# Three first-layer products split once more, Wq and Wk loaded by quarters, and a rebuilt adapter end in a one-core attention and MLP kernel

## The chip, the core and the metric

The kernel runs on one core of one Trainium2 chip. The metric is the device time of one execution in microseconds (us); a time below is in us unless it says otherwise. Engines are named as in the profile: PE is TensorE's matmul, PEld its weight load, DVE is VectorE, ACT is ScalarE, POOL is GpSimd, SP is SyncE (here it only issues DMAs). L1065 is line 1065 of the kernel before.

## What is computed

There are four sequences of 512 tokens with 512 features, all in float32. Cut to what matters, with `H = 2048`, `BN = 256` and one of three adapters chosen per sequence:

```python
q, k, v = x @ Wq, x @ Wk, x @ Wv
attn = softmax(q @ k.T * 512 ** -0.5)
attn_out = (attn @ v) @ Wp + bp
cms = gelu(attn_out @ cW1 + cb1) @ cW2 + cb2 + one_hot(code)      # 512 -> 2048 -> 512
mod = gelu(concat(attn_out, cms) @ mW1 + mb1) @ mW2 + mb2         # 1024 -> 2048 -> 512
y = clip(x + cms + mod, 0, 1)
h = y + gelu(y @ W_down[e] + b_down[e]) @ W_up[e] + b_up[e]       # adapter e of the sequence
out = (h - mean(h)) / sqrt(var(h) + 1e-5) * ln_w[e] + ln_b[e]
```

## The kernel before, in words

**Pairs and seven products.** The work goes by two pairs of sequences. Most products are done by a seven-product scheme (Strassen's in Winograd's form): the left operand is cut into four blocks, the right operand into four, seven products of sums of blocks take the place of eight, and the results are recombined by additions. In the MLP layers this is done at two levels: each of the seven outer products is itself done as seven. `FIRST_C`, `FIRST` and `SECOND` give the order of the outer products.

**The layer cW1** (`c1_layer`, L1035) has 512 features in and is only partly at two levels. Its outer products run in the order 2, 1, 5, 6, 7, 3, 4. Products 1 and 5 are done by `c1_two_level` (L990), which needs sums of weight blocks (the DRAM tensors `c1_inner`, made once by POOL in `expand_c1`, L217) and sums of token blocks (made on DVE in `c1_operands`, L960). Products 2, 6, 7, 3 and 4 are one-level: two groups of weights `g`, four tiles each, two matmuls of 128x128 by 512 columns per tile (L1065). The results of products 6 and 7 are put together per tile by `combine_first_tile` (L1078): two additions on DVE and a copy on ACT.

**The recombination inside a two-level product** is `seven` (L549). For each of two rows it holds sums in PSUM banks; there are eight banks in all, given out in turn. ACT copies the first product, DVE adds, and `keep` stores each of the four result blocks.

**Where the sums of weights come from.** POOL makes them while the first pair runs: `expansion` for cW1, cW2 and mW1 during attention, `late_expansion` for mW2 during pair 0's mW1 layer (L1131). They go to DRAM and come back through four weight slots `wslot`, which SP fills in the order of use (`fetch` L986, `inner_weights` L374).

**The second layers** (`second_layer`, L1189; matmuls L1215) need differences of blocks of the hidden values; `second_operands` (L1156) has DVE make them, half by half (`LOW`, `HIGH`), some of them beside the last products of the layer before (`after`).

**The start.** Wq and Wk come in by four row blocks each, on SP's and ACT's queues in turn (L120). PE turns all of Wq, then all of Wk (`transposed`, L411); ACT copies them out (L681, L641), DVE makes the eight block sums, and `folded` (L692) multiplies them by seven products (`small_product`, L652; matmuls L659). The first sequence's x is turned after that, and the first product with x is `pair_product` (L590; matmuls L595).

**The adapter** (`adapter`, L1307) is a generator, one step at a time between other work. PE turns the sequence back to rows (L1314), ACT copies it, POOL adds b_up; two down products with gelu follow (L1323, L1330), and then for each of four token tiles an up product (L1335), DVE's addition of the residual (L1343), statistics (L1345, L1347), the root on ACT (L1350), and the normalisation over ACT, DVE and POOL (L1352 to L1368). Pair 0's two adapters run between the products of pair 1's cW1 layer. Pair 1's second sequence runs around the last product of the last layer, its first sequence at the very end, so that nothing covers it.

**What sets the order.** Each engine works through its own list in order, and so do the DMA queues of SP, ACT and POOL. A scheduler places the instructions from the order of the code; `keep_in_program_order` pins some.

Of the kernel before, what the change touches and what calls it, by code (L numbers as in the profile page):

```python
# [18 lines left out]
def kernel(  # L19
# [38 lines left out]
    nc = tc.nc  # L58
# [64 lines left out]
    wq = weight((nc.sync, nc.scalar, nc.sync, nc.scalar), Wq, slot[0])  # L123
    wk = weight((nc.sync, nc.scalar, nc.sync, nc.scalar), Wk, slot[1])
# [12 lines left out]
    x_rows = [load_x(0, nc.scalar, x_places[0])]  # L137
    wv = weight((nc.scalar, nc.scalar), Wv, slot[2])
    x_rows.append(load_x(1, nc.sync, x_places[1]))
# [34 lines left out]


# [19 lines left out]
    def flat(t):  # L195
# [3 lines left out]

    c1_outer = [spill.tile([P, 3, 2, 2, 256], F32, name=f"c1_outer{u}") for u in range(2)]  # L200
    c1_inner = {
        (p, u): spill.tile([P, n], F32, name=f"c1_inner_{p}_{u}")
        for p, n in ((1, 1024), (5, 2048))
# [13 lines left out]
    def expand_c1(u, then):  # L217
# [23 lines left out]
        yield  # L241

# [43 lines left out]
    def expand(unit, raw, pairs, last, then):  # L286
# [40 lines left out]
        if last is not None:  # L327
            yield from plain((2, a12, one), (1, a11, three), (4, a22, two))
            tt(block(last), a12, s2, ALU.subtract)
            then()  # L330
            yield from full((5, one), (7, three), (6, two))
            yield from fourth(block(last), one)
        else:
            yield from plain((2, a12, one))
            tt(a12, a12, s2, ALU.subtract)
            yield from fourth(a12, three)
            yield from plain((1, a11, two), (4, a22, one))
            yield from full((5, one), (7, three), (6, two))
            then()

    def expand_all(units, raw, pairs, last):
        if last is None:
            load_raw(*units[0][:2], units[0][3], raw)
        for n, unit in enumerate(units):

            def then():
                if n + 1 < len(units):
                    load_raw(*units[n + 1][:2], units[n + 1][3], raw)

            yield from expand(unit, raw, pairs, last, then)  # L350
# [19 lines left out]
    def late_expansion():  # L370

        yield from expand_all(m2_units, slot[6:8], (flat(mod[0]), flat(mod[1]), slot[0]), None)
# [38 lines left out]
    def transposed(get, dst, finish=None):  # L411

        ps = [bank("tr_ps") for d in range(4)]
# [5 lines left out]
        for d in range(4):  # L419
            if finish is None:  # L420
                evacuate(dst[:, d, :], ps[d])
            else:
                finish(d, ps[d])
# [228 lines left out]
    def small_product(lhs, rhs, keep, then=None, copy=nc.scalar.copy):  # L652


        def matmuls(p, _, ps, first_):
# [14 lines left out]
            (1, 5, 6, 2, 7, 3, 4), then, copy,  # L670
# [5 lines left out]
    def left_from_psum(t, s):  # L676

        s1, s2, s3, s4 = (s[:, k] for k in range(4))

        def finish(d, ps):  # L680
            nc.scalar.copy(t[:, d, :], ps)  # L681
            c = d % 2
            if d < 2:
                minus(s3[:, c], ps[:, :256], t[:, c, 256:])
            else:
                minus(s2[:, c], ps[:, 256:], s3[:, c])
                add(s1[:, c], ps[:, 256:], t[:, c, 256:])
                minus(s4[:, c], ps[:, :256], s2[:, c])

        return finish  # L690

    def folded(lhs, rhs, w, s):  # L692
# [17 lines left out]
        small_product(lhs, rhs, keep)  # L710
# [71 lines left out]
    def first_operand(pair):  # L782
        xT, t_x = places(pair)
        transposed(chunks(x_rows[2 * pair]), xT[0], right_from_psum(xT[0], sums_in(flat(t_x[0]))))
# [17 lines left out]
    transposed(chunks(wq), wq_t, left_from_psum(wq_t, s_q))  # L802
    transposed(chunks(wk), wk_t, right_from_psum(wk_t, t_k))
    lhs_qk = folded(left_operand(wq_t, s_q), right_operand(wk_t, t_k), w_qk, sums_in(slot[0]))
    first_operand(0)
    load_bias()
    begun = both_operands(0)
    for pair in range(B // 2):
# [59 lines left out]
        if pair == 0:  # L868
            begun = {}
            then = {6: [lambda: first_operand(1)], 4: [lambda: begun.update(both_operands(1))]}  # L870
# [89 lines left out]
    def c1_operands(slots=(0, 1, 2, 3)):  # L960

        at0, at1, t12, t34 = (in_rows[i] for i in slots)
        b11, b12, b21, b22 = at0[:, 0:2, :], at1[:, 0:2, :], at0[:, 2:4, :], at1[:, 2:4, :]
        t1, t2, t3, t4 = t12[:, 0:2, :], t12[:, 2:4, :], t34[:, 0:2, :], t34[:, 2:4, :]

        def inner_sums(k, t):
            s = mod[1][:, 2 * k : 2 * k + 2, :].rearrange("p a (b n) -> p (a b) n", b=2)
            return inner_operands(t, 1, [s[:, i : i + 1, :] for i in range(4)], pinned=True)
# [4 lines left out]
        one = {1: inner_sums(0, b11)}  # L973
        minus(t1, b12, b11)

        def rest():
            one[5] = inner_sums(1, t1)
# [6 lines left out]
        return one, {2: b21, 3: b22, 4: t4, 6: t2, 7: t3}, rest()  # L984
# [5 lines left out]
    def c1_two_level(p, h, rhs):  # L990
# [3 lines left out]
        for g in range(2):  # L994
            w = next_weights()
            if p == 1:
                for m in range(2):
                    at = m * 512 + g * 256
                    fetch(
                        out=w[:, 512 * m : 512 * m + 512].rearrange("p (c n) -> p c n", c=2),  # L1000
                        in_=cW1[0:256, at : at + 256].rearrange("(c p) n -> p c n", p=P),
                    )
                fetch(out=w[:, 1024:], in_=c1_inner[1, g])
            else:
                fetch(out=w, in_=c1_inner[5, g])
# [17 lines left out]
        def keep(g, place, ps):  # L1023
            o, t = place
            tiles, tokens = slice(4 * o + 2 * g, 4 * o + 2 * g + 2), slice(256 * t, 256 * t + 256)
            nc.scalar.copy(h[2 if p == 1 else 3][:, tiles, tokens], halves_of(ps))
            if p == 1:
                done = h[0][:, tiles, tokens]
                add(done, halves_of(ps), done)

        seven(2, matmuls, keep, (1, 5, 6, 2, 7, 3, 4), at=mod[0])
# [3 lines left out]
    def c1_layer(h, rhs, after):  # L1035

        two_level, one_level, rest = rhs
        for p in FIRST_C:
            if p in (1, 5):
                c1_two_level(p, h, two_level[p])  # L1040
                yield
                continue
            for g in range(2):
                w = next_weights()
                if p in (2, 4):
                    k, o = {2: (1, 0), 4: (1, 1)}[p]
# [9 lines left out]
                else:  # L1056
                    s = {3: 2, 6: 0, 7: 1}[p]
                    a = w[:, :1024].rearrange("p (j c n) -> p j c n", j=2, c=2)
                    for j in range(2):
                        fetch(out=a[:, j], in_=c1_outer[j][:, s, g])  # L1060
                    lhs = lambda c, t, a=a: a[:, t // 2, c, (t % 2) * P : (t % 2 + 1) * P]
                for t in range(4):
                    ps = bank(f"c1_{p}")
                    for c in range(2):
                        nc.tensor.matmul(  # L1065
                            ps, lhsT=lhs(c, t), rhs=one_level[p][:, c, :],
# [8 lines left out]
                after(p, g)  # L1075
                yield
# [79 lines left out]
    def second_operands(h):  # L1156
# [19 lines left out]
        def after(p, g):  # L1176

            if (p, g) == (3, 1):
                differences(1, LOW)
                differences(3, LOW)  # L1180
# [4 lines left out]

        ready = []
        return operands, differences, after, ready

    def second_layer(made, src, kept_w, c, last, bias_c, beside):  # L1189

        operands, differences, _, ready = made
        c11, c12, c21, c22 = c
        rhs = ready[0]
        for i, p in enumerate(SECOND):
# [3 lines left out]
            if i == 0:  # L1198
                differences(3, HIGH)
# [92 lines left out]

    def load_adapter(b, w, aff):
        wd = w[:, : NV * BN].rearrange("p (c n) -> p c n", c=NV)
        wu = w[:, NV * BN : NV * BN + NB * V].rearrange("p (c n) -> p c n", c=NB)
        aff = aff[:, : 3 * V].rearrange("p (k n) -> p k n", k=3)
        bd = small.tile([P, NB], F32, name="bd")
        for c in range(NV):
            gathered(wd[:, c, :], wd_rows, idx_d[:, b, c : c + 1])
        for c in range(NB):  # L1300
            gathered(wu[:, c, :], wu_rows, idx_u[:, b, c : c + 1])
            gathered(bd[:, c : c + 1], bd_rows, idx_u[:, b, c : c + 1])
        for i, rows in enumerate((b_up, ln_w, ln_b)):
            gathered(aff[:, i, :], rows, idx_e[:, b : b + 1])
        return wd, wu, bd, aff

    def adapter(b, y, loaded, g, rows, eng, final=False):  # L1307

        wd, wu, bd, aff = loaded

        for t in range(NT):
            ps = bank("res_ps")
            for c in range(NV):
                nc.tensor.transpose(  # L1314
                    ps[:, c * P : (c + 1) * P], y[:, c, t * P : (t + 1) * P], ident
                )
            nc.scalar.copy(rows[:, t, :], ps)
# [198 lines left out]
```

## Time and profile before

| | us |
|---|---|
| median of 3 runs (1192.6 to 1193.76) | 1193.23 |
| the profiled execution, its own time | 1194.26 |
| its span, first to last instruction | 1192.5 |
| PE busy | 1168.9 |
| DVE busy | 883.5 |
| POOL busy | 482.7 |
| ACT busy | 294.9 |

The stages of the profiled execution, from its chain of waits: the start and the attention to about 248, the first cW1 layer from there to 346, cW2 to 431, mW1 to 602, mW2 to 686; then pair 1's cW1 layer with pair 0's adapters to 812, cW2 to 896, mW1 to 1065, mW2 with the second sequence's adapter to 1165, and the last adapter to the end. A row of the chain or of the order of time begins with its start and its length; a row of the waits has the total, the number of times and the longest; a row of groups has the count, the busy total and the mean of one in ns. An f32 matmul appears as two records. A granted clock of 1.00 is full speed.

### The profile page before, as it was taken

The numbers are of one execution on the slowest core, as the hardware profiler recorded it, in microseconds if no ns is written. First come the engines' busy times: TensorE is split into PE (matmuls) and PEld (weight loads), VectorE is DVE, ScalarE is ACT, GpSimd is POOL, SyncE is SP. The second block draws the span as 40 slices with busy tenths as digits, with TensorE's granted clock in tenths as the row PEclk, the third lists the DMA queues.
The fourth block names the chain that finished last, engine by engine and source line by source line (L and its number), as shares of the span: only waits on it lengthen the run. The fifth ranks groups of instructions, "written<-read, shape, count | busy, mean of one in ns | idle before, by whom it ended". The sixth has DMA issues, their size and how long they took to land.

```text
span 1192.5 us, 13167 instructions
## 1 busy us (share of the span) xinstructions
PE 1168.9 (98%) x4809; PEld 894.8 (75%) x4809; DVE 883.5 (74%) x1221; ACT 294.9 (25%) x540; POOL 482.7 (40%) x542
## 2 busy tenths in 40 slices
PE   7999999999999999999999999999999999999996
PEld 6478558747468888888888857447888888888872
DVE  4735565476789867897899837779894588699947
ACT  3234325335520000012310037551000002220014
POOL 4788999988940048870000522110000010124015
PEclk9999999999999999999999999999999999999998
DMA  8743695698756478787737553132735454775601
GB/s 289 277 149 135 245 351 196 218 389 331 262 194 249 176 279 319 283 293 251 241 134 297 177 177 133 54 132 106 293 131 187 166 211 168 219 240 187 228 1 71
DMA packets 78368, 251.50 MB, mean 211 GB/s; under 512 B 7348, under 2 KB 34016, under 8 KB 63456
## 3 DMA queue, kind: packets, MB, share of 16 engines
q1 hardware_dynamic: 54768, 149.96, 35.0%
q0 software_dynamic: 20736, 89.17, 21.2%
q10 hardware_dynamic: 2800, 11.54, 2.5%
q8 instruction: 38, 0.62, 0.2%
q14 instruction: 26, 0.21, 0.1%
HBM read 185.63 MB, written 65.01 MB: 210 GB/s over the span
## 4 chain that ended last, share of the span: by engine, by line
PE 92%; DMA 3%; DVE 2%; POOL 2%; ACT 1%; SPq 1%; issue 0%; ACTq 0%; DVEq 0%; POOLq 0%
PE i L1215 28%; PE i L1131 27%; PE c L1065 10%; PE sum L595 8%; PE sum L659 7%; PE sum L1014 4%; PE down_ps L1323 2%; PE up_ps L1335 2%; DMA wslot<-c_inner 1%; DMA wslot<-in_L_cond_mW 1%; PE tr_ps L416 1%; PE prod_ps L430 1%; PE res_ps L1314 1%; DMA wide<-in_L_cond_Wk 1%; SPq L988 1%
## 5 line engine op out<-in xcount | busy, mean ns | idle before, releaser
L1131 PE MATMUL i<-slot,wslot 128*128 128x256 f32 x1184 | 260.8, 379 | 0.0
L1131 PEld LDWEIGHTS i<-slot,wslot 128*128 128x128 f32 x1184 | 225.0, 190 | 30.6
L1215 PE MATMUL i<-slot,wslot 128*128 128x256 f32 x896 | 202.5, 379 | 0.0
L1215 PEld LDWEIGHTS i<-slot,wslot 128*128 128x128 f32 x896 | 170.2, 190 | 23.1
L906 ACT COPY first<-i 128x256 f32<-128x256 f32 (+1 forms) x56 | 26.8, 479 | 544.9 <-PE i L1215 280.6
L1215 PE MATMUL i<-hidden,wslot 128*128 128x256 f32 x576 | 132.2, 379 | 0.0
L899 DVE TENSOR_TENSOR part<-i,part 128x512 f32<-128x512 f32 (+1 forms) x156 | 90.9, 591 | 43.1 <-PE i L1131 26.6
L1215 PEld LDWEIGHTS i<-hidden,wslot 128*128 128x128 f32 x576 | 109.4, 190 | 16.2 <-issue 1.4
L928 ACT ACTIVATE hidden<-hidden,bias 128x512 f32<-128x512 f32 x128 | 85.2, 716 | 61.8 <-DVE hidden L505 60.7
L1065 PE MATMUL c<-slot,wslot 128*128 128x512 f32 x224 | 97.3, 592 | 0.0
L1065 PEld LDWEIGHTS c<-slot,wslot 128*128 128x128 f32 x224 | 42.5, 190 | 53.1 <-issue 50.5
L1286 POOL DMA_INDIRECT slot<-in_L_cond_W_down,idx_d x12 | 15.5, 1288 | 149.8 <-PE i L1215 88.2
L1286 POOL DMA_INDIRECT slot<-in_L_cond_b_up,idx_e x3 | 4.3, 1420 | 174.1 <-PE i L1131 173.5
L505 DVE TENSOR_TENSOR sum<-sum,wslot 128x512 f32<-128x512 f32 x51 | 35.4, 697 | 36.8 <-PE sum L659 18.7
L190 DVE TENSOR_TENSOR slot<-hidden,slot 128x1024 f32<-128x1024 f32 x48 | 58.4, 1217 | 0.3
L190 DVE TENSOR_TENSOR slot<-hidden 128x1024 f32<-128x1024 f32 x48 | 58.4, 1216 | 0.0
L899 DVE TENSOR_TENSOR part<-i,first 128x512 f32<-128x512 f32 (+1 forms) x62 | 36.3, 589 | 28.6 <-PE i L1131 16.2
L505 DVE TENSOR_TENSOR hidden<-c,hidden 128x512 f32<-128x512 f32 x64 | 43.3, 688 | 15.5 <-PE c L1065 14.3
L659 PE MATMUL sum<-hidden,wslot 128*128 128x256 f32 x232 | 53.5, 380 | 0.4 <-POOL wslot L180 0.4
L284 POOL DMA_DIRECT2D slot<-in_L_cond_mW x24 | 17.9, 753 | 81.4 <-DVE slot L190 80.5
L659 PEld LDWEIGHTS sum<-hidden,wslot 128*128 128x128 f32 x232 | 43.6, 190 | 6.8 <-POOL wslot L180 0.8
L505 DVE TENSOR_TENSOR hidden<-part,hidden 128x2048 f32<-128x2048 f32 x20 | 48.1, 2405 | 0.5
(307 smaller groups left out, 1988.6 us busy)
## 6 DMA issues: line engine op xcount, KB each, us to landing
wslot<-m_kept SPq DMA_DIRECT2D x48, 1024.0 KB
wslot<-m_kept SPq DMA_DIRECT2D x36, 512.0 KB
wslot<-c_kept SPq DMA_DIRECT2D x16, 1024.0 KB
slot<-in_L_cond_mW POOLq DMA_DIRECT2D x24, 512.0 KB
wslot<-in_L_cond_mW SPq DMA_DIRECT2D x24, 512.0 KB
slot<-in_L_cond_cW POOLq DMA_DIRECT2D x16, 512.0 KB
wslot<-in_L_cond_cW SPq DMA_DIRECT2D x32, 256.0 KB
m_kept<-wide POOLq DMA_DIRECT2D x6, 1024.0 KB
```

What stands on the lines that cost most here:

```text
L190: i = eng.tensor_tensor(out_, one, two, ALU.subtract)
L505: nc.vector.tensor_tensor(dst, a, b, ALU.add)
L595: nc.tensor.matmul(ps, lhsT=lhs[p][:, c, r * P : (r + 1) * P], rhs=rhs[p][:, c, :], start=(first_ and c == 0), stop=(c == 1), skip_group_c ...
L659: nc.tensor.matmul(v[:, j, :], lhsT=lhs[p][:, c, j * P : (j + 1) * P], rhs=rhs[p][:, c, :], start=(first_ and j == 0 and c == 0), stop=(c ...
L899: nc.vector.tensor_tensor(dst, ps, other, ALU.add)
L906: nc.scalar.copy(c1, p1)
L928: nc.scalar.activation(block[:, t, :], block[:, t, :], AF.Gelu, bias=bias_c[:, 8 * half + t : 8 * half + t + 1],)
L1014: nc.tensor.matmul(halves_of(ps)[:, j, :], lhsT=a[g][:, at_[q], j * P : (j + 1) * P], rhs=rhs[q][:, 0, :], start=(first_ and j == 0), stop ...
L1065: nc.tensor.matmul(ps, lhsT=lhs(c, t), rhs=one_level[p][:, c, :], start=(c == 0), stop=(c == 1),)
L1131: nc.tensor.matmul(out_ps[:, j, :], lhsT=a[j][q][:, c, :], rhs=now[q][:, c, :], start=(c == 0), stop=(c == 1),)
L1215: nc.tensor.matmul(ps[:, :256], lhsT=a[k // 2][q][:, k % 2, :], rhs=now[q][:, k, :], start=(k == 0), stop=(k == 3),)
L1323: nc.tensor.matmul(ps, lhsT=wd[:, c, n * P : (n + 1) * P], rhs=y[:, c, :], start=(c == 0), stop=(c == NV - 1),)
```

## The change

What it does, by parts:

- **Three more products at two levels**, in pair 1's cW1 layer only (`more`): 2, 6 and 7 beside 1 and 5. Sums of their weights are made in a second part of the late expansion, `expand_c1_late`. In pair 1 the token sums of all five are made on POOL instead of DVE, each ahead of its product (`prepare`). After product 6 or 7, DVE adds a block to h21 and POOL makes h12 or h22 from it. The adapters' steps are put inside the two-level products (`beside`).
- **The start**: Wq on SP's queue and Wk on ACT's, each by quarters of 256 rows and 256 columns. Each quarter of both is turned when it is there, and the products of the fold stand between the quarters, in the order 1, 2, 5, 6, 7, 3, 4; the first x is turned inside the fold. x, Wv and Wp follow on SP's queue. A tiny copy on ACT at the beginning (`touched`) calls for the activation table.
- **The adapters**: b_up is loaded as columns and added to y by ACT (`with_bias`). PE turns y in the up product's own bank, and the two up matmuls add to it, so that statistics and normalisation read PSUM. DVE subtracts the mean and multiplies by ln_w in one operation; ACT multiplies by the reciprocal root and POOL adds ln_b, or, for the last tiles, DVE does both in one.
- **The last adapter** goes by token halves: three of four half-width down products, the up products of tiles 0 and 1, the fourth down product, and tiles 2 and 3. The roots are pinned behind.
- **Half of one difference** of the second layers (`t1`, `LOW`) is made by ACT (a negated copy) and a DMA that adds, on POOL's queue, except in pair 0's cW1 layer; another (`t3`, `LOW`) moves to the second layer's beginning.
- In `expand` the next raw weights are loaded ahead of the last three blocks, and pair 0's mW1 layer takes three steps of the late expansion at a time instead of two.

The core of the diff:

```diff
-    wq = weight((nc.sync, nc.scalar, nc.sync, nc.scalar), Wq, slot[0])
-    wk = weight((nc.sync, nc.scalar, nc.sync, nc.scalar), Wk, slot[1])
+    QUARTERS = ((0, 0), (0, 1), (1, 0), (1, 1))
+    wq = quarters(Wq, slot[0], nc.sync)
+    wk = quarters(Wk, slot[1], nc.scalar)
...
+    def expand_c1_late(raws, sums):
+        units = [(p, u) for p in (2, 6, 7) for u in range(2)]
...
+        def rest():
+            for i, (p, u) in enumerate(units):
+                raw = block_of(i)
+                to = sums[i % 4].rearrange("p (k n) -> p k n", k=4)
+                weight_sums(
+                    raw[:, 0, 0], raw[:, 0, 1], raw[:, 1, 0], raw[:, 1, 1],
+                    *(to[:, k] for k in range(4)),
+                )
+                if i + 4 < len(units):
+                    load(i + 4)
+                nc.gpsimd.dma_start(out=c1_inner[p, u], in_=sums[i % 4])
+                yield
...
     def late_expansion():
-        yield from expand_all(m2_units, slot[6:8], (flat(mod[0]), flat(mod[1]), slot[0]), None)
+        spaces = (flat(mod[0]), flat(mod[1]), slot[0])
+        quarters = lambda tiles: [t[:, at : at + 1024] for t in tiles for at in (0, 1024)]
+        begin, rest = expand_c1_late(quarters(slot[6:8]), quarters(spaces[:2]))
+        yield from expand_all(m2_units, slot[6:8], spaces, None, begin)
+        yield from rest
...
-    transposed(chunks(wq), wq_t, left_from_psum(wq_t, s_q))
-    transposed(chunks(wk), wk_t, right_from_psum(wk_t, t_k))
-    lhs_qk = folded(left_operand(wq_t, s_q), right_operand(wk_t, t_k), w_qk, sums_in(slot[0]))
-    first_operand(0)
+    both_quarters(0, 0)
+    lhs_qk = folded(
+        lhs_q, rhs_k, w_qk, sums_in(slot[0]),
+        {
+            1: [lambda: both_quarters(0, 1), lambda: both_quarters(1, 0)],
+            2: [lambda: both_quarters(1, 1)],
+            6: [lambda: ends.append(first_operand(0))],
+            7: [lambda: ends[0]()],
+        },
+    )
...
         def keep(g, place, ps):
...
+            if p == 2:
+                nc.scalar.copy(h11, z)
+            elif p == 1:
+                nc.scalar.copy(h21, z)
+                add(h11, z, h11)
+            elif p == 5:
+                nc.scalar.copy(h22, z)
+            else:
+                add(h21, z, h21)
+                nc.gpsimd.tensor_tensor({6: h12, 7: h22}[p], h22, h21, ALU.add)
+            if p == 7 and place in ((0, 1), (1, 0)):
+                gelu(h[3], 1, cb1_c, (first_tile, first_tile + 1))
...
+        two = [p for p in FIRST_C if p in ((2, 1, 5, 6, 7) if more else (1, 5))]
...
+                ready[two[i]] = inner_sums(two[i], i % 2, nc.gpsimd if more else None)
...
+            if (p, g) == (3, 0) and not busy:
+                for two in (slice(0, 2), slice(2, 4)):
+                    tc.keep_in_program_order(
+                        nc.scalar.activation(t1[:, two, :], h11[:, two, :], AF.Copy, scale=-1.0)
+                    )
+            elif (p, g) == (3, 1):
...
+                    nc.gpsimd.dma_start(out=t1[:, LOW, :], in_=h12[:, LOW, :], accum_op=ALU.add)
...
+    def up(g, wu, y1, aff, h, t):
+        ps = bank("up_ps")
+        for c in range(NV):
+            nc.tensor.matmul(
+                ps[:, c * P : (c + 1) * P], lhsT=y1[:, c, t * P : (t + 1) * P], rhs=ident,
+                is_transpose=True, start=(c == 0), stop=True, skip_group_check=True,
+            )
+        for n in range(NB):
+            nc.tensor.matmul(
+                ps,
+                lhsT=g[:, n, t * P : (t + 1) * P],
+                rhs=wu[:, n, :],
+                start=False,
+                stop=(n == NB - 1),
+                skip_group_check=True,
+            )
...
+        nc.vector.scalar_tensor_tensor(h, ps, mv[:, 0:1], aff[:, 0, :], ALU.subtract, ALU.mult)
...
+    def normalised(b, h, mv, aff, t, eng, last=False):
+        rstd = small.tile([P, 1], F32, name="rstd")
+        root = nc.scalar.activation(rstd, mv[:, 1:2], AF.Sqrt, bias=eps)
+        if last:
+            tc.keep_in_program_order(root)
+        nc.vector.reciprocal(rstd, rstd)
+        if t == NT - 1 or last and t == NT - 2:
+            nc.vector.scalar_tensor_tensor(h, h, rstd, aff[:, 1, :], ALU.mult, ALU.add)
+        else:
+            nc.scalar.activation(h, h, AF.Copy, scale=rstd)
+            nc.gpsimd.tensor_tensor(h, h, aff[:, 1, :], ALU.add)
+        eng.dma_start(out=out[b, t * P : (t + 1) * P, :], in_=h)
...
+    def last_adapter(b, y, loaded, g, rows, y1, eng):
+        wd, wu, bd, bu, aff = loaded
+        with_bias(y, bu, y1)
+        first_half, second_half = slice(0, 256), slice(256, 512)
+        for n, tokens in ((0, first_half), (1, first_half), (0, second_half)):
+            down(y, wd, bd, g, n, tokens)
+        mvs = [up(g, wu, y1, aff, rows[:, t, :], t) for t in range(2)]
+        down(y, wd, bd, g, 1, second_half)
+        for t in range(NT):
+            if t > 1:
+                mvs.append(up(g, wu, y1, aff, rows[:, t, :], t))
+            normalised(b, rows[:, t, :], mvs[t], aff, t, eng, last=True)
```

## The prediction

> **What bounds the kernel now.** I read the page's busy times first, then what TensorE (PE) waits for, then the chain of waits, and last the order of time at both ends and around the first layer of pair 1.
>
> ```profile
> PE 1168.9 (98%) x4809; PEld 894.8 (75%) x4809; DVE 883.5 (74%) x1221; ACT 294.9 (25%) x540; POOL 482.7 (40%) x542
> ...
> PE tr_ps L416 <- DMA wide<-in_L_cond_Wq: 4.4, 1, 4.4
> PE sum L659 <- ACT hidden L641: 1.6, 1, 1.6
> PE i L1131 <- DMA wslot<-in_L_cond_mW: 1.3, 1, 1.3
> ...
> PE sum L1014 <- DVE sum L505: 0.9, 1, 0.9
> ```
>
> The columns of the waits are total, times and longest, in us. PE is busy for 1168.9 of 1192.5 us. Of the other 23.6, 4.4 is the wait for Wq, 1.6 the wait for its copies, some 11.4 comes after PE's last product (1181.1 to 1192.5), and about 6 is scattered. So only three things shorten this kernel: fewer PE passes, an earlier start, a shorter end. Work taken off VectorE (DVE) elsewhere is worth almost nothing, because DVE hardly ever holds PE up.
>
> **Three products at two levels.** The chain of waits prices both forms of a first-layer product.
>
> ```profile
> 686.29 6.87 PE c L1065 x16
> ...
> 698.34 6.87 PE c L1065 x16
> ...
> 710.61 12.09 PE sum L1014 x56
> ```
>
> The columns are start, length, what. Each f32 product is two records. A one-level product is two such groups of 16 records of 512 columns, 2 x 6.87 = 13.74 us; a two-level one is 56 records of 256 columns, 12.09 us. Products 2, 6 and 7 of pair 1 change over: 3 x 1.65 = 4.9 us of PE removed, on the path. The transposes of the adapters stay as many (16 each), the downs and ups too.
>
> What the new form asks of the others, by its rows: product 6 or 7 needs 8 DVE adds inside the recombination and 8 into h21, 16 x 0.69 = 11.0 us, as much as the 16 adds of its one-level form did, in 1.65 us less. With its share of the adapter (bn_stats 0.69, aggregate 0.18, subtract-and-scale 0.99, reciprocal 0.15 = 2.0 per token tile, against 2.7 before) product 7 loads DVE with 11.0 + 2 x 2.0 = 15.0 us beside 12.09 + 2 x 2.15 = 16.4 us of PE. DVE is covered, by little. POOL gets 8 adds of 1.27 us for each of products 6 and 7 (L1368's row, 128x512) and 4 sums of 0.72 us ahead of each two-level product: 13 of 16 us. By the order of the built kernel the sums for products 2 and 1 stand ahead of the 16 large adapter gathers on POOL's queue, so product 2 does not wait behind some 26 us of gathers (664.6 to 690.4 before). Behind POOL's adds wait DVE's next adds into h21, and ScalarE's (ACT's) gelu of h22; that is due only two products (27 us) later. With 8 banks, the next product's second bank is that of this product's last sum but one; between them lie two to four us of adapter products, except after products 2 and 1. I charge 0.9 us, the size of the one such wait in the rows above. Net **-4.0**; bounds -6.4 (the 1.45 us that PE loses today in 686 to 811 goes too) and 0.
>
> **The start.** Now all of Wq and Wk land before PE can multiply.
>
> ```profile
> 4.39 3.64 PE L416 MATMUL tr_ps<-ident,wide 128*128 128x128 f32 x16 [4.39 <-DMA wide<-in_L_cond_Wq]
> ...
> 8.20 2.92 PE L416 MATMUL tr_ps<-ident,wide 128*128 128x128 f32 x16 [0.16 <-DMA wide<-in_L_cond_Wk]
> ...
> 8.82 1.28 ACT L681 ACT_TABLE_LOAD   x1 [8.82 <-DMA wide<-in_L_cond_Wk]
> ...
> 12.71 2.05 PE L659 MATMUL sum<-hidden 128*128 128x256 f32 x8 [1.59 <-ACT hidden L641]
> ...
> 28.79 3.60 PE L595 MATMUL sum<-hidden,cms 128*128 128x512 f32 x8
> ```
>
> The quarters are the same 2 MB at the same 385 GB/s or so (1 KB rows instead of 2 KB; the cW1 loads with 1 KB rows ran in the stretch at 388). The first pair should land at 4.4, the last near 8.1. The table load (1.28) moves into the wait. Then, in PE's order: 8 transposes at the early 0.23 us, to 6.2; the copies, 0.7, to 6.9; product 1, 8 records at 0.2 to 0.4, to about 9.7; 16 transposes at 0.11 to 0.15, to 11.6; a copy; product 2, 1.73, to 13.7; the last 8 transposes, 0.9, to 14.6; product 5 behind one add of 0.7, and then 5 products (8.6) with x's transposes (1.75 and 1.75) and the bias, to 27.3. The sums (512 wide, 0.69 each, 8 of them) stay ahead from product 6 on. So the pair product starts at 27.3 instead of 28.8: **-1.5**. Bounds: 0, and -5.1 if PE ran from 4.39 with no wait at its later rate (64 x 0.109 + 12.1 + 0.3 = 19.4). x now follows Wq on SP's queue, Wv and Wp behind it; Wv is needed at 46 and Wp at 56 us, 4 MB at 385 GB/s are in by 19. The savings carry through the attention: POOL's chain there (0.4 us of PE waits) starts earlier too, since x lands sooner than today's 16.5 us.
>
> **The end.** PE's work after the last product is unchanged in sum, so its end stays where it is on before's scale, 1181.1.
>
> ```profile
> 1179.09 0.73 ACT L1350 ACTIVATE rstd<-mv,eps 128x1 f32<-128x1 f32 x2
> ...
> 1182.94 0.98 DVE L1352 SCALAR_TENSOR_TENSOR hidden<-hidden,mv,wide 128x512 f32<-128x512 f32 x1
> ...
> 1184.03 1.56 DVE L1356 SCALAR_TENSOR_TENSOR hidden<-hidden,rstd,wide 128x512 f32<-128x512 f32 x1
> ...
> 1185.51 1.74 DVE L1367 TENSOR_TENSOR hidden<-hidden,wide 128x512 f32<-128x512 f32 x1
> ...
> 1188.01 0.33 SPq L1369 DMA_DIRECT2D out<-hidden  x1
> ```
>
> Today the last output is issued 6.9 us after PE's end, and lands 4.5 us later. In the new order the last gelu ends two ups (4.3 us) before PE's end, less 0.7, at 1177.5; the root's table load 1.28, to 1178.8; the roots and scales of tiles 0 and 1 (2 x 1.1), to 1181.0; DVE then does tile 2 (0.69 + 0.18 + 0.99 + 0.15, and about 1.0 for the last), largely behind PE's end, to 1183.2, and tile 3, 2.8, to 1186.0. The residual's add, the shift and one of two affine passes are gone. SP issues at 1186.1: **-2.0**. Bounds -4.0 (tile 2 fully hidden) and 0 (ACT's order makes DVE wait: the roots now stand behind all four gelus).
>
> **The rest.** Pair 0's m1 layer (431 to 602 us) gets POOL's late sums for cW1: 24 x 0.72 = 17 us, 18 DMA issues of 0.6 and some landings, so POOL ends near 565 instead of 533; the next use of its buffers, the sums at 589, has 24 us left. Some 16 more small gathers (columns of b_up), 1.3 us each, fall into POOL's idle 342 to 422. Half of t1 done by ACT and an adding DMA: no cost; it can start near 580, after product 3's gelus, and the sums that read it come after 605. But POOL and DVE disturb each other. The first row is a DVE group beside POOL in 440 to 460 (mean 3,378 ns, where two more of the same shape took 722), the second a POOL addition beside DVE at 524, and the third gives the busy time of PE, PEld, DVE, ACT and POOL in 20 us:
>
> ```profile
> L190 DVE TENSOR_TENSOR slot<-slot,slot 128x512 f32<-128x512 f32 x2 | 6.8, 3378 | 0.0
> ...
> 523.77 2.77 POOL L180 TENSOR_TENSOR wide<-wide 128x256 f32<-128x256 f32 x1
> ...
> 500.00:520.00 20.00, 20.00 (x94) 17.62 (x93) 19.79 (x20) 1.17 (x2) 17.28 (x19) 1.00 0.68 241
> ```
>
> DVE is full there and PE still runs through. 533 to 565 would be such a stretch. From both sides: 0, and 17 us of POOL less some 11 us in which DVE is idle there now, 6.5. I take **+0.5**, near what the rows of 440 to 520 show.
>
> The Trainium skill speaks against moving adds to POOL: "SBUF — State Buffer", section "SBUF: two separate sides", says that a DVE operation with two SBUF inputs and a GpSimd operation that reads SBUF exclude each other for a whole instruction. The 3,378 ns row agrees. The 16 adds into h21 read PSUM and one SBUF tile, and at 731.55 POOL's add took 1.26 us beside such adds of 0.69; by the rule taken for all adds the sum of the first layer would be near zero, by the row it is -4.0.
>
> **Sum**, against the profiled execution's own 1194.26 us (span 1192.5): -4.0 - 1.5 - 2.0 + 0.5 = -7.0, 1187.3. That execution is 1.0 above the median of the runs, 1193.23, from which the forecast is **1186.2**.
>
> **Rivals.**
> - *POOL becomes the bound in products 6 and 7* (slower). 16 adds, begun 9 us into product 6, against 37.5 us of PE there and 13.7 of product 3 before product 4 writes h21: PE waits once an add takes over (37.5 + 13.7 - 9)/16 = 2.6 us, and the whole gain is gone at 3.1. At 1.27 + 2.05, the delay of the 2.77 us row, it is 3.3: 11 us late, 1197. For it: that row. Against it: 1.26 beside PSUM adds. Chance 0.08.
> - *DVE locked out in m1 of pair 0* at the full 6.5: 1192.2. For it: DVE full at 500 to 540; against it: PE at 20.00 of 20 there. 0.08.
> - *The ends do not give*: the quarters land late or DVE's chain at the end is as long as now, so only the passes count: 1189.7. 0.12.
> - *The bounds the other way* (start -4, no new wait): 1181. 0.08.
> - The forecast, 1183 to 1189: 0.64.
>
> Range 1181.5 to 1191.2: it leaves out most of the first two rivals and the better half of the fourth. 0.2% of the time, 2.4 us, is about what a measurement of this kernel can tell: faster (under 1190.8) 0.64 + 0.08 + 0.10, same 0.02 + 0.07, slower 0.09.
>
> **What would show it.** Right: PE's passes in the first layer of pair 1 end 4 us sooner after their start; the pair product starts at 27.3; the last output is issued some 5 us after PE's last product; no new wait of PE in 533 to 602. Wrong: POOL adds of h12 and h22 above 2.6 us, PE waiting for DVE at the start of products 5, 6 or 7, or DVE waiting for roots at the end.

## The result, and the profile after

The changed kernel takes **1198.39 us** (median of 6 runs, 1194.56 to 1199.45) against 1192.73 for the kernel before beside it: a ratio of 1.0041, 95% interval 1.0026 to 1.0057. It is slower by some 5 us; 1186.2 was forecast, with a range up to 1191.2. The profiled execution took 1197.96, with a span of 1196.2.

In the changed kernel the matmuls of the layer mW1 are at L1277, those of the second layers at L1375, the two-level products of cW1 at L1134, the fold at L733, the first pair product at L667. The busy times from its page, and then PE's waits (total, times, longest):

```profile
PE 1166.5 (98%) x4897; PEld 912.5 (76%) x4897; DVE 872.1 (73%) x1186; ACT 295.4 (25%) x536; POOL 544.9 (46%) x613
```

```profile
PE i L1277 <- DMA wslot<-in_L_cond_mW: 12.3, 4, 5.9
PE tr_ps L869 <- DMA wide<-in_L_cond_Wq: 4.3, 1, 4.3
PE sum L1134 <- DMA wslot<-c_inner: 1.1, 1, 1.1
PE sum L733 <- DVE wslot L577: 1.0, 1, 1.0
PE sum L733 <- DVE hidden L882: 0.9, 1, 0.9
```

PE is busy for 2.4 us less, and yet the span is longer: the first row was 1.3 before and is 12.3 now, 10.8 of it in pair 0 and 1.5 in pair 1. PE waits for raw blocks of mW1 that SP fetches into its weight slots. The chain of waits puts the place; pair 0's mW1 layer before, and then in the changed kernel:

```profile
430.86 96.71 PE i L1131 x448
527.59 14.22 DMA wslot<-in_L_cond_mW
541.80 0.04 issue
541.85 59.84 PE i L1131 x276
```

```profile
428.18 132.97 PE i L1277 x616
561.15 0.02 issue
561.16 24.87 DMA wslot<-in_L_cond_mW
586.04 0.04 issue
586.08 25.69 PE i L1277 x108
611.77 84.61 PE i L1375 x392
```

The mW1 layer of pair 0 now lasts from 428.18 to 611.77, 183.6 us instead of 170.8. The marks of the two chains, stage by stage, account for the whole difference (us; the layers left out, cW2 of both pairs and mW2 of pair 0, take 84.6 each in both):

| stage | before | after | difference |
|---|---|---|---|
| to the start of mW1, pair 0 | 430.9 | 428.2 | -2.7 |
| mW1, pair 0 | 170.8 | 183.6 | **+12.8** |
| cW1, pair 1, with pair 0's adapters | 125.2 | 118.9 | **-6.4** |
| mW1, pair 1 | 169.2 | 171.7 | +2.5 |
| mW2, pair 1, and the end | 127.1 | 124.6 | -2.5 |
| span | 1192.5 | 1196.2 | +3.7 |

What happens in mW1 of pair 0 is seen in three orders of time of the changed kernel. POOL's queue, from the end of the late sums:

```profile
559.51 0.56 POOL L296 DMA_DIRECT2D c_inner<-mod  x1
...
562.48 0.57 POOL L296 DMA_DIRECT2D c_inner<-mod  x1 [0.30 <-POOL mod L195]
563.04 0.94 POOL L1604 DMA_DIRECT2D cms<-xT_kept  x1
569.13 0.85 POOL L1335 DMA_DIRECT2D wide<-hidden  x1 [5.15 <-ACT wide L1328]
571.79 0.85 POOL L1604 DMA_DIRECT2D cms<-xT_kept  x1 [1.81 <-PE i L1277]
```

SP's queue (two blocks in one row, issued at 560.30 and 561.16):

```profile
560.30 1.56 SPq L448 DMA_DIRECT2D wslot<-in_L_cond_mW  x2
```

And PE:

```profile
571.33 1.89 PE L1277 MATMUL i<-slot,wslot 128*128 128x256 f32 x8
579.16 2.05 PE L1277 MATMUL i<-slot,wslot 128*128 128x256 f32 x4 [5.94 <-DMA wslot<-in_L_cond_mW]
586.08 6.27 PE L1277 MATMUL i<-slot,wslot 128*128 128x256 f32 x18 [4.87 <-DMA wslot<-in_L_cond_mW]
```

Each of the last three POOL rows adds 1 MB to what lies in SBUF (x to cms twice, h12 to t1), and two 512 KB stores of the late sums stand right in front of them. Before, the two additions to cms were issued 24 us apart, with nothing of POOL's between:

```profile
551.92 0.91 POOL L1419 DMA_DIRECT2D cms<-xT_kept  x1 [18.69 <-PE i L1131]
576.10 0.87 POOL L1419 DMA_DIRECT2D cms<-xT_kept  x1 [23.27 <-PE i L1131]
```

Now five transfers start within 12.3 us, and PE gets the two blocks that SP issued at 560.30 and 561.16 only at 579.16 and 586.04, 19 and 25 us later. The windows show the DMA engines and the clock (busy time and count of PE, PEld, DVE, ACT and POOL, then granted clock, DMA share, GB/s); the first row is a stretch with full DMA engines elsewhere in this kernel:

```profile
250.00:270.00 20.00, 18.80 (x57) 10.37 (x56) 16.52 (x14) 5.38 (x10) 15.81 (x16) 1.00 1.01 407
...
575.00:580.00 5.00, 0.84 (x2) 0.78 (x3) 1.27 (x1) 0.00 (x0) 0.00 (x0) 0.67 1.02 223
580.00:585.00 5.00, 1.21 (x3) 0.40 (x2) 0.00 (x0) 0.00 (x0) 0.00 (x0) 0.50 1.01 241
585.00:590.00 5.00, 3.92 (x9) 3.20 (x10) 0.00 (x0) 1.75 (x4) 0.00 (x0) 0.50 0.96 352
```

The DMA engines are full and yet move only 223 and 241 GB/s in 575 to 585; in 250 to 270 us, as full, they move 407. The granted clock falls to half while PE waits, so the matmuls behind the waits are slow too: 4 records took 2.05 us and 18 took 6.27, where 8 take 1.89. That makes 10.8 us of waits and some 3.5 us of slow matmuls.

### The profile page after: what moved, and what is told of

It is laid out like the page before. It is cut to its first block, busy times and chain, and to the rows that moved or that the text cites. A ratio compares the mean times of both kernels' runs of the same rounds, so it can differ in the third digit from the quotient of the medians.

```text
span 1196.2 us, 13426 instructions
## 1 busy us (share of the span) xinstructions
PE 1166.5 (98%) x4897; PEld 912.5 (76%) x4897; DVE 872.1 (73%) x1186; ACT 295.4 (25%) x536; POOL 544.9 (46%) x613
## 4 chain that ended last, share of the span: by engine, by line
PE 91%; DMA 6%; ACT 1%; DVE 1%; SPq 1%; issue 0%
PE i L1375 28%; PE i L1277 25%; PE sum L733 8%; PE sum L667 8%; PE c L1209 7%; PE sum L1134 7%; DMA wslot<-in_L_cond_mW 3%; PE down_ps L1481 2%; PE up_ps L1500 2%; PE tr_ps L484 1%; DMA wslot<-c_inner 1%; PE prod_ps L502 1%; DMA wslot<-m_kept 1%; SPq L1103 1%; PE up_ps L1495 1%; PE tr_ps L869 0%
## 5 line engine op out<-in xcount | busy, mean ns | idle before, releaser
L1277 PE MATMUL i<-slot,wslot 128*128 128x256 f32 x1184 | 264.8, 382 | 12.3 <-DMA wslot<-in_L_cond_mW 12.3
L1277 PEld LDWEIGHTS i<-slot,wslot 128*128 128x128 f32 x1184 | 226.7, 192 | 45.3 <-issue 6.3
L1375 PE MATMUL i<-slot,wslot 128*128 128x256 f32 x896 | 202.5, 379 | 0.0
L1375 PEld LDWEIGHTS i<-slot,wslot 128*128 128x128 f32 x896 | 170.2, 190 | 23.1
L1375 PE MATMUL i<-hidden,wslot 128*128 128x256 f32 x576 | 132.1, 379 | 0.0
L1375 PEld LDWEIGHTS i<-hidden,wslot 128*128 128x128 f32 x576 | 109.4, 190 | 16.2 <-issue 1.4
L1446 POOL DMA_INDIRECT slot<-in_L_cond_ln_w,idx_e x3 | 5.3, 1770 | 156.7 <-PE i L1277 156.1
L1209 PE MATMUL c<-slot,wslot 128*128 128x512 f32 x160 | 69.2, 592 | 0.0
L1209 PEld LDWEIGHTS c<-slot,wslot 128*128 128x128 f32 x160 | 30.4, 190 | 38.3 <-issue 35.6
L204 DVE TENSOR_TENSOR slot<-hidden 128x1024 f32<-128x1024 f32 x48 | 59.4, 1237 | 0.0
L733 PE MATMUL sum<-hidden,wslot 128*128 128x256 f32 x232 | 53.2, 379 | 0.0
L1134 PE MATMUL sum<-mod,wslot 128*128 128x256 f32 x224 | 52.0, 379 | 1.1 <-DMA wslot<-c_inner 1.1
L577 DVE TENSOR_TENSOR hidden<-part,hidden 128x2048 f32<-128x2048 f32 x20 | 52.7, 2635 | 0.5
L733 PEld LDWEIGHTS sum<-hidden,wslot 128*128 128x128 f32 x232 | 43.8, 190 | 5.8
L1134 PEld LDWEIGHTS sum<-mod,wslot 128*128 128x128 f32 x224 | 42.5, 190 | 7.2 <-issue 1.5
```

The source lines that it names most:

```text
L204: i = eng.tensor_tensor(out_, one, two, ALU.subtract)
L577: nc.vector.tensor_tensor(dst, a, b, ALU.add)
L733: nc.tensor.matmul(v[:, j, :], lhsT=lhs[p][:, c, j * P : (j + 1) * P], rhs=rhs[p][:, c, :], start=(first_ and j == 0 and c == 0), stop=(c ...
L1134: nc.tensor.matmul(halves_of(ps)[:, j, :], lhsT=a[g][:, at_[q], j * P : (j + 1) * P], rhs=rhs[q][:, 0, :], start=(first_ and j == 0), stop ...
L1209: nc.tensor.matmul(ps, lhsT=lhs(c, t), rhs=operands[p][:, c, :], start=(c == 0), stop=(c == 1),)
L1277: nc.tensor.matmul(out_ps[:, j, :], lhsT=a[j][q][:, c, :], rhs=now[q][:, c, :], start=(c == 0), stop=(c == 1),)
```

## The experiments

Theory A: the DMA engines are crowded by the adding DMAs and the late stores, and SP's weight fetches land late. Theory B: the late sums of cW1 alone do it. Theory C, from the prediction: POOL and DVE hold each other up, and PE waits for DVE. Times are medians; ratios are against the kernel before. Numbers for mW1 are those of pair 0 and pair 1.

**e1: t1 on DVE.** `second_operands` as before, in all layers:

```diff
     def second_operands(h, busy=False):
+        busy = True
```

> The changed kernel with t1's LOW half made by DVE in all layers, as before: the negated copy on ACT and the adding DMA are gone, and t3's LOW half is back beside product 3. Theory A (crowding: in mW1 of pair 0 the six late stores of cW1 sums, the two additions of x to cms and the adding DMA of t1 are issued between 540 and 572 us, the DMA engines are full from 560 to 590, and SP's mW1 blocks land late): one MB of the three adding ones goes, so PE's 10.8 us of waits in mW1 of pair 0 fall to 3 to 6, that layer lasts 175 to 178 instead of 183.6, mW1 of pair 1 goes back from 171.7 to 169.2 to 169.5, and the kernel takes 1186 to 1190. Theory B (the late sums of cW1 alone hold PE up, the adding DMA is harmless): mW1 of pair 0 stays at 182 to 184, pair 1's at 171 to 172, the kernel at 1196 to 1198. Theory C (VectorE and POOL exclude each other, and PE waits for VectorE): PE's waits name VectorE, and get longer, since VectorE has more to do.

Measured: 1188.62, ratio 0.9962 (0.9939 to 0.9986). mW1 lasts 173.5 and 169.7, and PE's wait for mW1 is 2.4 us. That is what A said, and somewhat more. B, the late sums alone, falls as the whole cause, and so does C for this layer, since PE's waits in it name only the DMA. With t1 on DVE, though, PE waits 1.9 us for DVE in pair 1's first layer, which lasts 121.0 instead of 118.9.

**e2: no more products at two levels**, and no late sums; the adding DMA stays.

```diff
-        for _ in c1_layer(h, c1_rhs, made[2], final, lambda: steps(extra, 1)):
-            if not final:
-                steps(between, 2)
+        for _ in c1_layer(h, c1_rhs, made[2], False, lambda: steps(extra, 1)):
+            steps(between, 2)
...
-        yield from expand_all(m2_units, slot[6:8], spaces, None, begin)
-        yield from rest
+        yield from expand_all(m2_units, slot[6:8], spaces, None)
```

> The changed kernel without the three products at two levels: 2, 6 and 7 of pair 1 are one-level again, token sums are on DVE, and the late sums of cW1 are not made. The adding DMA of t1 stays. Theory A: without the late stores POOL reaches the additions to cms at 550 and 573 us, but the adding DMA of t1 still falls beside the second one, as in pair 1: mW1 of pair 0 lasts 171.5 to 174, pair 1's 171 to 172, the first layer of pair 1 is back at 125, and the kernel takes 1192 to 1195. Theory B: mW1 of pair 0 is back at 170.8 or less, and the kernel takes 1190 to 1192. Theory C: as B for pair 0; pair 1's mW1 stays at 171.7.

Measured: 1195.00, ratio 1.0017 (1.0001 to 1.0034). mW1 lasts 172.9 and 173.7; PE waits for mW1's blocks five times, 5.2 us in all. So the adding DMA of t1 alone takes all that the start and the end gain. In pair 1 it is even dearer than in the changed kernel.

**e3: both left out**, so that the start, the adapters and the end remain.

> Both left out: no more products at two levels, no late sums of cW1, t1's LOW half on DVE. What stays of the change is the start by quarters, the rebuilt adapters and the last adapter by token halves. By theory A and B alike mW1 lasts 170.8 and 169.2 as before, the first layer of pair 1 125, and what is left is the gain of the start and the attention (2.7) and of the end (2.4): 1187 to 1189. If the adapters' 16 small gathers or the other changed parts cost something of their own, it is above 1190.

Measured: 1188.88, ratio 0.9969 (0.9954 to 0.9984). mW1 lasts 169.2 in both pairs, without a wait. The four corners for mW1, pair 0 and pair 1: neither 169.2, 169.2 (e3); t1's DMA alone 172.9, 173.7 (e2); the late sums alone 173.5, 169.7 (e1); both 183.6, 171.7. In these executions each alone costs about 4 us in pair 0, both together 14.4: the two fill the same queue at the same time. The medians say it more weakly: t1's DMA costs 6.1 without the late sums (e2 against e3) and 9.8 beside them (the changed kernel against e1).

**e4: the same adding DMA later.** Nothing is taken out.

```diff
-            if (p, g) == (3, 0) and not busy:
+            if (p, g) == (4, 0) and not busy:
                 ...
-                else:
-                    nc.gpsimd.dma_start(out=t1[:, LOW, :], in_=h12[:, LOW, :], accum_op=ALU.add)
...
             elif (p, g) == (4, 1):
+                if not busy:
+                    nc.gpsimd.dma_start(out=t1[:, LOW, :], in_=h12[:, LOW, :], accum_op=ALU.add)
                 differences(1, HIGH)
```

> The changed kernel with nothing taken out, but the negated copy for t1 made after the first half of product 4 (not 3), and so the adding DMA some 12 us later: after the second addition to cms instead of ahead of it in pair 0. Theory A: the adding DMAs no longer stand next to each other, so mW1 of pair 0 lasts 174 to 179, pair 1's 169 to 170.5, and the kernel takes 1186 to 1191. If it is the number of bytes and not their place: no difference, 1197 to 1199. Theory B: no difference in pair 0. Against the move: the second product of the second layers reads t2, made from t1; if the DMA lands later than some 12 us into that layer, DVE waits for it and PE for DVE.

Measured: **1186.21**, ratio 0.9938 (0.9915 to 0.9962). mW1 lasts 170.8 and 169.8, shorter in pair 0 than A expected; PE waits there for no block, only 1.4 us for DVE. POOL's queue in this kernel:

```profile
562.21 0.94 POOL L1603 DMA_DIRECT2D cms<-xT_kept  x1
578.16 0.85 POOL L1603 DMA_DIRECT2D cms<-xT_kept  x1 [15.01 <-PE i L1277]
599.51 0.85 POOL L1337 DMA_DIRECT2D wide<-hidden  x1 [20.49 <-ACT wide L1328]
```

All bytes are still moved; only the three additions now stand 16 and 21 us apart. So the same bytes cost next to nothing in another place. (Not all of the 16 us is due to the edit: see the end of this section.) The windows of 560 to 590 us, in the changed kernel and then in e4:

```profile
560.00:590.00 30.00, 19.19 (x75) 15.67 (x74) 11.44 (x12) 6.79 (x11) 5.37 (x8) 0.78 1.02 281
```

```profile
560.00:590.00 30.00, 30.00 (x141) 26.41 (x139) 20.98 (x23) 8.85 (x14) 3.71 (x6) 1.00 0.94 283
```

The bytes per second are the same, 281 and 283 GB/s; in e4 more of them are SP's (4.81 MB of 8.48, against 4.15 of 8.42), and PE runs through.

**e5: e4 with the start of the kernel before** (row blocks, `transposed(chunks(wq), ...)`, the old queues).

> The version with t1's adding DMA behind product 4 (e4), with the start of the kernel before: Wq and Wk by row blocks on two queues, all of both turned before the fold, x and Wv on the queues they had, no early table load. Theory of the prediction (the quarters let the pair product start 1.5 us sooner): 1.5 slower than with the quarters, 1187.7 at 1186.2 for e4. Theory from the marks of the five executions with the quarters (pair product at 28.8 to 30.4, against 28.8 before): the quarters give nothing or cost up to 1.5, and this version takes 1184.7 to 1186.2, with the pair product at 28.8.

Measured: 1188.64, ratio 0.9964 (0.9948 to 0.9980), so 2.4 slower than e4, but the intervals overlap. The pair product begins at 28.0, sooner than with the quarters. Neither expectation covers both; e10 repeats the question.

**e6: e2 with a copy in place of the addition**, so that t1 lacks its subtraction.

```diff
-                    nc.gpsimd.dma_start(out=t1[:, LOW, :], in_=h12[:, LOW, :], accum_op=ALU.add)
+                    nc.gpsimd.dma_start(out=t1[:, LOW, :], in_=h12[:, LOW, :])
```

> e2 (no more products at two levels, t1's LOW half by ACT and a DMA) with the DMA copying instead of adding, so t1 is h12 and not h12 minus h11. Same 1 MB at the same place in POOL's queue. If an adding DMA takes the engines for longer than its bytes (it must read what it adds to), mW1 of pair 1 falls from 173.7 to 170 to 171.5 and PE's waits for mW1's blocks from 5.2 to under 3 us. If only the bytes count, the layer stays at 172 to 174.

Measured: 1189.02, ratio 0.9971 (0.9954 to 0.9989), 6 us better than e2 with as many bytes; mW1 lasts 171.1 and 169.4, and PE waits 1.5 us for its blocks instead of 5.2. The DMA view of 1032 to 1056 us gives POOL's queue, q0 (packets, MB, share of 16 engines), in e3 with the second addition to cms alone:

```profile
q0 software_dynamic: 144, 1.05, 23.1%
```

in e2 with that and the addition to t1:

```profile
q0 software_dynamic: 288, 2.10, 47.7%
```

and in e6 with the addition to cms and a copy to t1:

```profile
q0 software_dynamic: 288, 2.10, 34.4%
```

Of 24 us these shares are 5.5, 11.4 and 8.3. So 1 MB added holds all 16 engines for 5.5 to 5.9 us, 1 MB copied for 2.7: **an adding DMA costs twice a copy of the same bytes**.

**e7: e4 without the three products** and without their late sums.

> e4 without the three products and without their late sums: t1's adding DMA behind product 4, nothing else beside the start, the adapters and the end. If the three products are worth what their layer shows (125.3 against 118.9), it takes 6.4 more than e4: 1192.6 at 1186.2. If their late sums cost elsewhere (POOL's 17 us and 18 DMAs in mW1 of pair 0), less: 1189 to 1190, close to e3's 1188.9. mW1 of pair 0 and 1 should last 169.2 to 170 in either case.

Measured: 1189.73, ratio 0.9974 (0.9958 to 0.9989). Against e4, the three products with their late sums are worth 3.5 us by medians. Their layer gives 5.4 (124.3 to 118.9). What becomes of the other 2 isn't located by this pair: in the profiled executions mW1 of pair 0 is longer in e7 than was expected (172.7 against 169.2 to 170, with 2.1 us of waits for its blocks and 0.7 for DVE), while e4's PE waited 3.0 us for a block of cW1 in pair 0's first layer, where e7's waited 1.9.

**e8: t1 on POOL**, by one subtraction, with no DMA and no negated copy.

```diff
-                    nc.gpsimd.dma_start(out=t1[:, LOW, :], in_=h12[:, LOW, :], accum_op=ALU.add)
+                    nc.gpsimd.tensor_tensor(
+                        t1[:, LOW, :], h12[:, LOW, :], h11[:, LOW, :], ALU.subtract
+                    )
```

> The changed kernel with t1's LOW half made by one POOL subtraction of 128 x 2048 at the place where the adding DMA is issued, and no negated copy on ACT: no engine but POOL is touched, POOL is idle there, and 1 MB of adding DMA is gone. Theory A (the DMA engines): mW1 of pair 0 lasts 170.8 to 174 (the two additions to cms are still closer together than before, at 563 and about 573), pair 1's 169.2 to 170, the first layer of pair 1 119 to 121, and the kernel takes 1185 to 1188. Rival (POOL beside DVE is what costs): the subtraction of some 5 us makes DVE's operations on hidden up to 5 us longer, PE waits for DVE at the beginning of the second layers, and it takes 1189 or more.

Measured: **1185.17**, ratio 0.9937 (0.9912 to 0.9961); mW1 lasts 170.9 and 169.6, the first layer of pair 1 118.9. The subtraction:

```profile
570.27 4.53 POOL L1330 TENSOR_TENSOR wide<-hidden,hidden 128x2048 f32<-128x2048 f32 x1 [10.24 <-ACT hidden L1033]
```

DVE's operations beside it, with one operand from PSUM, did not stretch:

```profile
570.39 0.69 DVE L1004 TENSOR_TENSOR part<-i,part 128x512 f32<-128x512 f32 x1
571.33 1.42 DVE L1004 TENSOR_TENSOR part<-i,part 128x512 f32<-128x512 f32 x2 [0.25 <-PE i L1277]
```

Of the versions with three more products, e8 and e4 cannot be told apart.

**e9: the changed kernel with a copy in place of the addition**, the edit of e6.

> The changed kernel, with the DMA into t1 copying instead of adding (t1 is h12, not h12 minus h11); everything else as it is. In e2 and e6 an adding MB cost the 16 engines some 5 to 6 us and a copied one 2.7. By that the queue of 540 to 590 us is shorter by 2.5 to 3 us: PE waits 5 to 8 us instead of 10.8, mW1 of pair 0 lasts 176 to 180 instead of 183.6, pair 1's 169.2 to 170, and the kernel takes 1187 to 1192. If the addition itself doesn't matter in this crowd, 1196 to 1198.

Measured: 1190.13, ratio 0.9977 (0.9945 to 1.0009). The four runs fall into two groups, 1186.4 and 1186.7, 1193.6 and 1193.8; the profiled execution is of the first. In it mW1 lasts 173.0 and 169.6, and PE waits 1.8 us for a block at 530 and for none between 545 and 603. The time is within what was expected. By how much the copy shortens the queue in the crowd, this profile doesn't show, because POOL was done 5 us sooner in it (see below).

**e10: e8 with the start of the kernel before.**

> The version with t1's LOW half on POOL (e8, 1185.17), with the start of the kernel before: a second measurement of what the quarters are worth, since e5 against e4 (1188.64 and 1186.21) has intervals that overlap. If the start is worth what the prediction said (1.5) or what e5 showed (2.4), 1186.7 to 1187.6, with the pair product at 28.0 to 28.8 and the end of pair 0's first layer 1 to 2.5 later than e8's 345.1; if it is worth nothing, 1184.5 to 1185.8.

Measured: 1186.35, ratio 0.9932 (0.9909 to 0.9954). By medians 1.2 slower than e8, by the ratios no slower; pair 0's first layer ends at 344.4, sooner than e8's 345.1, where 1 to 2.5 later was expected if the quarters gain. mW1 of pair 0 took 175.8 in its profiled execution, with 3.5 us of waits, though it is the layer of e8: one execution of a crowded stage can differ by 5 us from another.

**Two courses of POOL.** Until some 560 us the changed kernel, e4, e8 and e9 run the same program, and yet POOL issues the last late store 134.3 us after the start of mW1 in the changed kernel and 128.7 to 128.9 in the other three. The courses part near 490 us, at one DVE operation beside POOL's sums; in the changed kernel and then in e4:

```profile
489.38 3.35 DVE L577 TENSOR_TENSOR hidden<-part,hidden 128x2048 f32<-128x2048 f32 x1
```

```profile
494.13 6.66 DVE L577 TENSOR_TENSOR hidden<-part,hidden 128x2048 f32<-128x2048 f32 x1
```

Where it took 6.7 to 6.8 us (e4, e8, e9), PE waited 1.4 to 1.5 us for DVE, POOL was done sooner, the two additions to cms stood 16 to 18 us apart, and PE waited for no block of mW1 beside them. Where it took 3.4 to 3.7 (the changed kernel, e1, e5, e10), the last late store came 134.3 to 135.8 us into the layer, the additions stood 7 to 9 us apart, and PE waited for blocks. What decides between the two isn't shown. So a fair comparison of this layer stays within one course. In the second it took 183.6 us with t1's addition between the other two (the changed kernel), 171.6 with that addition 24 us behind them (e5, with the old start), and 173.5 and 175.8 with none (e1, e10). The place of that one DMA is what costs, then, and the runs agree: all six of the changed kernel took 1194.6 or more, all five of e4 1188.0 or less, all six of e8 1190.2 or less.

## Why the prediction was wrong, step by step

- **The rest, +0.5: the step that failed.** It measured +12.8 and +2.5. Two sentences did it. "Half of t1 done by ACT and an adding DMA: no cost" weighed when t1 would be needed, and not that 1 MB added takes the 16 engines for over 5 us beside SP's fetches; nor did the prediction ask what stands beside it in pair 1. It had this DMA starting near 580; it was issued at 569.13, between the two additions to cms. And the late sums were priced as POOL time, "18 DMA issues of 0.6 and some landings". POOL did end near 565, as predicted (its last store is issued at 562.48). But that delay moved the first addition to cms from 551.9 to 563.0, against t1's and the second one. Bounds of 0 to 6.5 were taken from POOL and DVE, the wrong resource. The row of 1.3 us for mW1's blocks, shown in the prediction, was a sign: one of these fetches came late even before, at 541.8.
- **Locked-out DVE, the rival for this stage**, didn't come in the changed kernel, where PE's waits in mW1 name only the DMA. In e4, e8 and e9 it came, at 1.4 to 1.5 us of the 6.5. The rival of the right sign in this stage had the wrong cause, and the true one was not among the rivals.
- **Three products, -4.0**: the mechanism was right, the size was -6.4, the bound given. PE has no wait at all in that layer of the changed kernel; the 0.9 us charged for one was not due. e3, without the products, splits it: 0.9 comes with the rebuilt adapters (125.2 to 124.3), 5.4 with the products. POOL's additions, the condition of the first rival, stayed at 1.30:

```profile
L1158 POOL TENSOR_TENSOR hidden<-hidden,hidden 128x512 f32<-128x512 f32 x16 | 20.5, 1296 | 13.7 <-DVE hidden L577 13.6
```

- **The start, -1.5**: the pair product was to begin at 27.3.

```profile
4.33 1.94 PE L869 MATMUL tr_ps<-ident,wide 128*128 128x128 f32 x8 [4.33 <-DMA wide<-in_L_cond_Wq]
7.14 3.44 PE L733 MATMUL sum<-hidden 128*128 128x256 f32 x8 [0.87 <-DVE hidden L882]
...
16.18 3.72 PE L733 MATMUL sum<-wslot,wslot 128*128 128x256 f32 x16 [1.02 <-DVE wslot L577]
...
28.75 3.60 PE L667 MATMUL sum<-hidden,cms 128*128 128x512 f32 x8
```

It began at 28.75 here, and at 29.7 in the mean of the nine profiled executions with quarters (28.8 to 30.3), against 28.8, 28.0 and 28.3 with the old start. Product 1 took 3.44 us for 8 records, 0.43 each and not the 0.2 to 0.4 that the prediction assumed; the two waits for DVE, 0.9 and 1.0, were a little over the 0.7 that it allowed for each; and its own terms from product 5 on (8.6, 1.75, 1.75 and the bias) add up to 12.3, not to the 12.0 that led to 27.3. From the pair product to the end of that stage PE then wins back 1.1 (26.0 against 27.1), so both starts are level there: 55.7 in the mean of the nine, 55.5 of the three. Nor is the -2.7 of the table all the start's: mW1 of pair 0 begins at 430.2 in the mean of the nine (428.2 to 432.9), and at 430.9, 432.7 and 429.0 with the old start. By the runs the start is worth 2.4 (e5 against e4) or 1.2 (e10 against e8) by medians, 3 or nothing by ratios: small, and not settled. The five longest of e5's twelve runs have a lower granted clock (0.993 to 0.995, the others 0.996 to 0.998), so that a part of the 2.4 may be waits in mW1; no profile of such a run is there to show it.

The Trainium skill, "TensorE: Matmul & The Clock Gate", section "Part 1: The HAM clock gate (the "warmup" mystery)", says that after an idle window PE runs at half rate until it has been busy for some 3.4 us, and that the window runs freely, so that the cold stretch varies from run to run. The rate agrees: 8 records of product 1 took 3.44 to 3.75 us, and 8 of the same shape take 1.89 later. The length doesn't: here the slow records reach from 4.3 to 10.4, over 6 us, with one wait of 0.9 between. And the granted clock of these windows reads 1.00. So it isn't shown that the clock made product 1 slow. In the new order the slow stretch falls on products, in the old one mostly on transposes.

- **The end, -2.0**: right, -2.5. The span from PE's last record (1187.2) to the end is 9.0 us instead of 11.4. The wait for the roots that the prediction named as a bad sign was there (DVE idle for 2.14 us), on the chain that ended last; but its sum had the roots at that place, after the last gelu and the table load, and held:

```profile
1184.70 0.29 ACT L1518 ACTIVATE rstd<-mv,eps 128x1 f32<-128x1 f32 x1
...
1185.03 0.16 DVE L1521 RECIPROCAL rstd<-rstd 128x1 f32<-128x1 f32 x1 [2.14 <-ACT rstd L1518]
...
1190.78 0.75 DVE L1523 SCALAR_TENSOR_TENSOR hidden<-hidden,rstd,wide 128x512 f32<-128x512 f32 x1
```

DVE ends at 1191.5, and the last output goes 4.4 us after PE's end, where some 5 were predicted.

Without the one neglected DMA, the forecast would have stood: e4 and e8 differ from the changed kernel only in how or when half of t1 is made, and take 1186.2 and 1185.2. They beat both kernels. That the number fits so well is partly luck: the products gave 6.4 instead of 4.0, and the start little or nothing instead of 1.5.

## What to carry to other kernels

Price a DMA that a change adds, or moves, by the time it holds the shared DMA engines, in the window where it will run, beside the fetches that PE lives on; a queue that issues it for free says nothing. A wait of 1 us for weights in the profile before is a warning that the fetches of that layer have little slack, though another fetch than that one may be hit. When work on a DMA-issuing engine gets longer, list every transfer queued behind it and see whom it meets. Before comparing one stage of two profiles, see that they took the same course up to that stage.

## What the runs showed of the hardware

- 1 MB added by a DMA into SBUF held the 16 DMA engines for 5.5 to 6.0 us (e3 and e2; 42.9% of the 14 us from 598 in e4), 175 to 190 GB/s; 1 MB copied from SBUF to SBUF for 2.7 (e6), some 390 GB/s.
- Waits of 5.9 and 4.9 us took the granted clock from 1.00 to 0.50, and it was back at 0.96 in the window of 590 to 595: some 3.5 us lost besides 10.8 of waiting.
- SP's fetches and POOL's transfers share one resource: SP's blocks issued at 560.30 and 561.16 landed 19 and 25 us later, while POOL's queue held 59.4% of the engines between 560 and 590.
- One DVE operation of 128x2048 took 2.28 us at 511.7 in e8, and 6.74 at 490.9 beside POOL's sums.

The Trainium skill, "DMA: Bandwidth & Descriptors", section "Issuing engines are not separate DMA queues", says just this: DMAs started by different engines run on the same 16 DMA engines and interleave. The rows above agree.
